# A two-layer graph network on one core: query blocks of 496 and 351, more products on GpSimd, second products split by columns

## The chip, the core and the metric

The kernel runs on one core of a Trainium2 chip. The metric is the device time of one execution in microseconds, the median of three runs. The engines are called by the profile's names: PE (TensorE, matrix products; PEld is its weight load), DVE (VectorE), ACT (ScalarE), POOL (GpSimd) and SP (SyncE, which here issues DMAs).

## The reference

There are N = 3327 nodes with D = 128 features and a dense 0/1 adjacency matrix `adj`. Layer 0 is a graph convolution with batch norm. Layer 1 is an attention in which the roles are unusual: each of the 128 columns d of the projections, reshaped, is an attention of its own with a head size of 8 over all 3327 nodes, and twice the adjacency matrix is added to the scores.

```python
h = jnp.maximum(_layernorm(x), 0.0)
x = x + layer0(h, adj)           # adj.T @ h / deg, two weights, batch norm, relu
h = jnp.maximum(_layernorm(x), 0.0)
q = (h @ Wq.T).reshape(d, n, 8)  # k and v likewise; d = 128, n = 3327
a = jnp.einsum('dnh,dmh->dnm', q, k) * d ** -0.5 + adj + adj
out = jnp.einsum('dnm,dmh->dnh', softmax(a, axis=2), v)
return x + out.reshape(n, 8 * d) @ Wo.T
```

So 128 attentions of 3327 x 3327 scores are computed, and nearly all the time is spent there.

## The kernel before

**Front.** The first 290 us compute layer 0, all in one pool of SBUF tiles (`l0`): 26 loads of rows of `adj` with seven products each, batch norm, `residual`, the second norm (`roots`, `factors`, `second_norm`, `columns`) and the projections of the first four heads (`project_now`). After these stand the loads of k, v and q of the first group; q goes over ACT's DMA queue (L578), k is sorted by casts on POOL and ACT (L581). Three early blocks of weights exp(2 adj + low) are made for the chunks from WC = 19 on (L433, `weigh_early`) and written to DRAM as `wd`.

**Attention.** NG = 32 groups of G = 4 columns d. A group goes over seven blocks of queries (six of 512 and one of 255), and a block over the 26 chunks of 128 keys. A chunk has two halves, each with two of the four heads, so a block has 52 pairs (chunk, half). They are handled in SU = 13 steps of four pairs. A pair's product `s` (L725) is two matrix products of K = 32 into one PSUM tile of two banks; there are three such tiles (`psc`). A pair is finished in one of two ways:

- plain (38 a block): DVE adds the adjacency tile to `s` (L818, `add`) into one part of the tile `d`; the whole `d` of a step, three pairs, is exponentiated by ACT one step later (L856, `late`).
- weighted (14 a block): ACT exponentiates `s` directly (L828), and POOL multiplies the result `f` with the weights from `wd` (L831).

A step has three plain pairs and a weighted one; the last has two of each. Three steps later (LAG) the second products (L604, `weigh`) multiply the exponentials with v and gather in the PSUM tile `av`. They are fp32, with 9 columns each, and four of them for four heads stand in the four column groups of PE; each shows as two records. `second(0)` issues the couple of the first two pairs, `second(1)` that of the others. The order on PE, written out by hand, is in each step: weighted product, first plain product, `second(0)`, a part of `finish` (the end of the block before), second and third plain product, `beside`, `second(1)`.

**Beside the loop.** `beside` puts nine parts of side work into the steps of each group: six projections for a later group (`projection`) and three parts of the output of the group before (`outputs`). Each has a PE part (steps 7 and 10), an evacuation by DVE (8 and 11) and a last part (9 and 12). `more_weights` makes the weights of the blocks from 3 on within the first group. `loads` spreads the loads of the next group's q, k and v over SP's queue and its sorting casts over POOL.

Which of the three `s` tiles a product takes is settled when the program is built: the one that is expected to be free first. Names of the engines' waits in the built program show the choice.

Of the kernel before, what the change touches and what calls it, by code (L numbers as in the profile page):

```python
# [44 lines left out]
def tile_two_layer_gnn(  # L45
# [21 lines left out]
    }))  # L67
    blocks = [(n0, min(NB, N - n0)) for n0 in range(0, N, NB)]

    const = ctx.enter_context(tc.tile_pool(name="const", bufs=1))  # L70
# [57 lines left out]

    def q_loads(q, p0, d):

        qs = qT[:, bass.ds(d * N, NP)].rearrange("(a h) n -> a h n", h=H)
        return [(q[p0 + i * H : p0 + (i + 1) * H].bitcast(F32), qs[i // 2]) for i in range(4)]

# [152 lines left out]
    with tc.tile_pool(name="l0", bufs=1) as l0, tc.tile_pool(  # L286
# [50 lines left out]
        def roots(c0, c1):  # L337
            nc.scalar.activation(sd[:, c0:c1], mv[:, c0:c1, 1], AF.Sqrt, bias=eps)
# [93 lines left out]
        weights = []  # L432
        for y, (n0, w) in enumerate(blocks[:EARLY]):  # L433
            a = ap.tile([P, 7 * NB], F32, name="a")
            a7 = a.rearrange("p (c n) -> p c n", c=7)
            nc.sync.dma_start(a7[:, :, :w], adjr[:, WC:, n0 : n0 + w])
            weights.append((a7, n0, w))

        def weigh_early():
            a7, n0, w = weights.pop(0)  # L440
            nc.scalar.activation(a7[:, :, :w], a7[:, :, :w], AF.Exp, bias=low, scale=2.0)
            nc.sync.dma_start(
                wd[:, :, n0 : n0 + w].rearrange("c p n -> p c n"), a7[:, :, :w]
            )

# [71 lines left out]
        def residual(i):  # L517
            pt, cs = turned(i, A, acc[i])
            nc.vector.tensor_add(xs[:, cs, :], xs[:, cs, :], pt)
            nc.sync.dma_start(  # L520
                xd.rearrange("(c p) d -> p c d", p=P)[:, cs, :], xs[:, cs, :]
            )

# [52 lines left out]
        for i in range(4, NQ):  # L576
            relu(i)
        for b in range(G):  # L578
            for args in q_loads(q, 32 * b, b):
                nc.scalar.dma_start(*args)  # L580
        for x, c in enumerate(range(0, NC, 4)):  # L581
            n = min(4, NC - c)
            (nc.scalar.copy if x % 2 else nc.gpsimd.tensor_copy)(
                k[:, c : c + n, :],
                ks.bitcast(F32).rearrange("g (p c) -> g c p", c=NC)[:, c : c + n, :],
            )
# [10 lines left out]
        keep_columns(0, NQ)  # L597
        weigh_early()

# [9 lines left out]
    def finish(rp, av, d0, n0, w):  # L609

        avs = rp.tile([P, NB], F32, name="avs")
        nc.vector.tensor_copy(avs[:, :w], av[:, :w])  # L612
        yield

        J = 4 if w == NB else 3
# [36 lines left out]
    def attention():  # L652


        with tc.tile_pool(name="adj", bufs=4) as ap, tc.tile_pool(
# [17 lines left out]
            if True:  # L673
                steps = [
                    (i, y, s)
                    for i in range(NG) for y in range(len(blocks)) for s in range(SU)
                ]
# [4 lines left out]
                def pairs(s):  # L682


                    last = s == SU - 1
                    plain = [(j // 2, j % 2) for j in range(3 * s, 3 * s + 3 - last)]
                    rest = [(WC + s // 2, 1 - s % 2)]
                    return plain, rest + ([(NC - 1, 0)] if last else [])


                wanted, have = [], {}
                for x, (i, y, s) in enumerate(steps):
                    n0, w = blocks[y]
# [4 lines left out]
                    c = pairs(s)[1][0][0]  # L698
                    if (1, i, y, c) not in have:
                        have[1, i, y, c] = None  # L700
                        wanted.append((x, 1, i, y, c))

                def fetch(x):
                    while wanted and wanted[0][0] <= x:
                        _, kind, i, y, c = wanted.pop(0)
                        n0, w = blocks[y]
                        if kind:
# [10 lines left out]
                def product(i, y, c, half):  # L718
                    q, k, _ = sets[i % 2]
                    n0, w = blocks[y]  # L720
                    we = w + w % 2
# [8 lines left out]

                waiting, ending, pending = [], [], []
                late = None

                def more_weights(i, y, s):

                    k, phase = s // 3, s % 3
                    if i or y + 1 >= len(blocks) or y + 1 < EARLY or k > 3:
                        return
                    n0, w = blocks[y + 1]
                    c = WC + 2 * k  # L740
# [33 lines left out]
                extra = []  # L774

                def second(part):

                    (i, y, s), es = waiting[0]
                    n0, w = blocks[y]
                    av = avs2[(i * len(blocks) + y) % 2]  # L780
# [8 lines left out]
                    if part:  # L789
                        waiting.pop(0)  # L790
                        if s == SU - 1:
                            ending.append(finish(rp, av, at(i), n0, w))

# [5 lines left out]
                for x, (i, y, s) in enumerate(steps):  # L799
                    n0, w = blocks[y]  # L800
                    fetch(x + PRE)
                    k = x - i * SU * len(blocks) - FROM[i]
# [4 lines left out]
                    while pending and (total - len(pending)) * (SU * len(blocks) - FROM[i] - 4) <= k * total:  # L807
# [42 lines left out]
                    beside(i, y, s)  # L850
                    if due:
                        second(1)

# [4 lines left out]
                    waiting.append(((i, y, s), es))  # L858
                late()
                while waiting:  # L860
                    second(0)
                    step()
                    second(1)
                while ending:
# [6 lines left out]
    def attention_shifted():  # L871

        with tc.tile_pool(name="shq", bufs=1) as shp, tc.tile_pool(
# [11 lines left out]
            with tc.For_i(0, D, G) as d0:  # L885
# [3 lines left out]
                for b in range(G):  # L889
# [3 lines left out]
                    )  # L893
                for y, (n0, w) in enumerate(blocks):
                    we = w + w % 2
# [168 lines left out]
```

## Time and profile before

| | us |
|---|---|
| median of three runs (10510.94 to 10513.17) | 10511.22 |
| profiled execution, as timed | 10527.91 |
| its span in the profile | 10526.1 |
| first DVE addition of the attention | 298.15 |
| start of one wide block's copy of `av` to that of the next (L612), without and with two parts of side work | 46.95 and 48.33 |
| one group (five starts of L612 from 4953.84 to 5271.93, seven blocks apart) | 318.09 |
| DMA, mean busy share of 16 engines in that group | 57% |
| granted PE clock, mean | 0.986 |

A line of the timeline has a start, a length (both in us), the engine, the line of the code, the operation, output and input tiles with their shapes, and how many equal instructions were merged; the brackets hold idle time before it and what ended it. A pipelined engine starts an instruction before the one ahead has fully ended, so what an instruction costs its engine is read from start to start. PE records' ends are modelled.

### The profile page before, as it was taken

The numbers are of one execution on the slowest core, as the hardware profiler recorded it, in microseconds if no ns is written. First come the engines' busy times: TensorE is split into PE (matmuls) and PEld (weight loads), VectorE is DVE, ScalarE is ACT, GpSimd is POOL, SyncE is SP. The second block draws the span as 40 slices with busy tenths as digits, with TensorE's granted clock in tenths as the row PEclk, the third lists the DMA queues.
The fourth block names the chain that finished last, engine by engine and source line by source line (L and its number), as shares of the span: only waits on it lengthen the run. The fifth ranks groups of instructions, "written<-read, shape, count | busy, mean of one in ns | idle before, by whom it ended". The sixth has DMA issues, their size and how long they took to land. (4 is left out here: it accounts for less than half of the span.)

```text
span 10526.1 us, 186778 instructions
## 1 busy us (share of the span) xinstructions
PE 9922.7 (94%) x72399; PEld 2813.8 (27%) x72399; DVE 9714.9 (92%) x9949; ACT 9948.5 (95%) x6200; POOL 7497.1 (71%) x3868
## 2 busy tenths in 40 slices
PE   7889999999999999999999999999999999999999
PEld 3222222222222222222222222222222222222222
DVE  5789999999999999999999999999999999999998
ACT  4889999999999999999999999999999999999998
POOL 0667777777777777777777777777777777777776
PEclk8899999999999999999999999999999999999999
DMA  7655555555555555555555555555555555555554
GB/s 241 192 168 163 157 168 165 163 162 160 162 166 165 164 162 157 161 170 163 160 162 157 165 170 165 160 158 163 164 169 163 162 163 158 165 165 167 156 152 128
DMA packets 1115761, 1731.67 MB, mean 165 GB/s; under 512 B 198350, under 2 KB 441932, under 8 KB 1107180
## 3 DMA queue, kind: packets, MB, share of 16 engines
q1 hardware_dynamic: 1110478, 1713.99, 56.3%
q8 instruction: 568, 9.31, 0.4%
q10 hardware_dynamic: 4350, 5.64, 0.2%
q14 instruction: 333, 2.73, 0.1%
q0 software_dynamic: 32, 0.00, 0.0%
HBM read 1618.76 MB, written 100.53 MB: 163 GB/s over the span
## 5 line engine op out<-in xcount | busy, mean ns | idle before, releaser
L818 DVE SCALAR_TENSOR_TENSOR d<-at,s 128x1024 f32<-128x1024 f32 x8512 | 9204.3, 1138 | 642.7 <-PE s L725 406.2
L831 POOL TENSOR_TENSOR f<-f,wt 128x1024 f32<-128x1024 f32 (+1 forms) x3136 | 6983.8, 2235 | 2619.1 <-ACT f L828 2572.0
L856 ACT ACTIVATE d<-d 128x3072 f32<-128x3072 f32 (+1 forms) x2912 | 7372.9, 2532 | 73.4 <-DVE d L818 70.5
L604 PE MATMUL av<-d,v 128*9 128x512 f32 x34048 | 5528.5, 569 | 0.1
L725 PE MATMUL s<-q,k 32*128 32x512 f32 x23296 | 4280.7, 482 | 505.7 <-DVE d L818 218.0
L725 PEld LDWEIGHTS s<-q,k 32*128 32x128 f32 x23296 | 1773.9, 182 | 5829.2 <-DVE d L818 3312.2
L828 ACT ACTIVATE f<-s 128x1024 f32<-128x1024 f32 (+1 forms) x3136 | 3014.8, 970 | 313.8 <-PE s L725 252.3
L604 PE MATMUL av<-f,v 128*9 128x512 f32 x12544 | 2864.0, 571 | 0.0
L604 PEld LDWEIGHTS av<-d,v 128*9 128x9 f32 x34048 | 630.7, 88 | 1381.6 <-issue 1265.4
L604 PEld LDWEIGHTS av<-f,v 128*9 128x9 f32 x12544 | 310.6, 88 | 52.9 <-issue 41.0
L180 POOL CAST k<-ks 128x256 fp32r<-128x256 f32 x434 | 284.2, 655 | 0.0
L416 PE MATMUL acc<-a,A 128*128 128x512 f32 (+1 forms) x364 | 151.3, 568 | 24.0 <-ACT A L350 23.3
L619 PEld LDWEIGHTS av<-ident,avs 128*128 128x128 f32 (+1 forms) x864 | 121.1, 208 | 179.9 <-issue 178.8
L226 POOL TENSOR_TENSOR o<-pf,o 104x512 fp32r<-104x512 f32 x124 | 160.4, 1293 | 9.9
L619 PE MATMUL av<-ident,avs 128*128 128x128 f32 (+1 forms) x864 | 163.8, 311 | 0.6 <-DVE avs L612 0.6
L225 POOL CAST o<-pf 104x512 fp32r<-104x512 f32 x124 | 75.8, 611 | 115.3 <-DVE pf L224 59.8
L612 DVE COPY avs<-av 128x512 f32<-128x512 f32 (+1 forms) x224 | 144.2, 644 | 2.8 <-PE av L604 2.8
L423 DVE TENSOR_REDUCE amax<-a 128x1 f32<-128x3327 f32 x26 | 93.7, 3610 | 37.7 <-DMA a<-in_adj 37.7
L416 PEld LDWEIGHTS acc<-a,A 128*128 128x128 f32 x364 | 68.8, 192 | 108.8 <-issue 84.4
L420 ACT ACTIVATE junk<-a 128x3327 bf16<-128x3327 f32 x26 | 77.4, 2977 | 6.6 <-DMA a<-in_adj 6.5
L389 POOL TENSOR_TENSOR sq<-wk 128x512 f32<-128x512 f32 x2 | 2.1, 1040 | 102.3 <-PE aside L390 102.3
L629 DVE TENSOR_TENSOR oq<-av,ri 128x128 f32<-128x128 f32 (+1 forms) x224 | 64.1, 286 | 7.7
(120 smaller groups left out, 952.0 us busy)
## 6 DMA issues: line engine op xcount, KB each, us to landing
at<-in_adjT SPq DMA_DIRECT2D x1728, 512.0 KB
wt<-wd SPq DMA_DIRECT2D x1344, 256.0 KB
at<-in_adjT SPq DMA_DIRECT2D x288, 255.0 KB
ks<-kT SPq DMA_DIRECT2D x496, 104.0 KB
q<-qT SPq DMA_DIRECT2D x496, 104.0 KB
at<-in_adjT SPq DMA_DIRECT2D x192, 256.0 KB
a<-in_adj SPq DMA_DIRECT2D x26, 1663.5 KB
wt<-wd SPq DMA_DIRECT2D x224, 127.5 KB
```

What stands on the lines that cost most here:

```text
L180: nc.gpsimd.tensor_copy(k[:, c : c + n, half * 64 : half * 64 + 64], ks.bitcast(F32).rearrange("g (p c) -> g c p", c=NC)[:, c : c + n, :],)
L226: nc.gpsimd.tensor_tensor(o[:CH, 1], f[:CH], o[:CH, 0].bitcast(F32), ALU.subtract)
L416: nc.tensor.matmul(acc[i][:, :w], A[:, c, :], a[:, n0 : n0 + w], start=(c == 0), stop=(c == NC - 1),)
L423: nc.vector.tensor_reduce(amax[:, c : c + 1], a[:, :N], AX.X, ALU.max, apply_absolute_value=True)
L604: nc.tensor.matmul(av[32 * b : 32 * b + H + 1, :w], tiles[2][:, b, c, :], e, start=first, stop=last,)
L612: nc.vector.tensor_copy(avs[:, :w], av[:, :w])
L619: nc.tensor.transpose(pt[:R, j, :], avs[:, j : j + (R - 1) * J + 1 : J], ident)
L725: nc.tensor.matmul(p[:, x, :we], k[rs, c, :], q[rs, n0 : n0 + we], start=True, stop=True,)
L818: nc.vector.scalar_tensor_tensor(d[:, j, :, :w], have[0, i, y, c // 2][:, c % 2, :w] .unsqueeze(1).to_broadcast([P, 2, w]), SAFE / 2, p[:, ...
L828: nc.scalar.activation(f[:, :, :w], p[:, :, :w], AF.Exp, scale=2.0)
L831: nc.gpsimd.tensor_tensor(f[:, :, :w], f[:, :, :w], have[1, i, y, c][:, :w].unsqueeze(1).to_broadcast([P, 2, w]), ALU.mult,)
L856: nc.scalar.activation(flat, flat, AF.Exp, scale=2.0)
```

## The change

- Queries go in blocks of QB = 496, so six of 496 and one of 351 (`qblocks`) instead of six of 512 and one of 255. Layer 0 keeps its blocks.
- WC is 18: 16 of the 52 pairs are weighted and 36 plain. Steps 4, 8 and 12 (`DOUBLE`) have two weighted pairs, the others one.
- A couple of second products is split by columns into two halves of 248 where a block is wider than `NARROW` = 400. The first half of the first couple stands where that couple stood; its second half and both halves of the second couple stand behind the step's last product.
- Front: only one block's weights are made early, in two halves; the others are made in the first group by `more_weights`. Only the first 512 queries are loaded in front; the rest of q is loaded by SP, two DMAs a step, in the first eight steps (`others`). The sorting casts of k stand behind `columns`, the last `weigh_early` moved up, and `xs` is stored once instead of in seven parts.
- Side work: the PE part in steps 7 and 11, the evacuation in 8 and 12, the last part in 9 or in step 0 of the next block.

```diff
+QB = 496
-WC = 19
+WC = 18
-EARLY = 3
+DOUBLE = (4, 8, 12)
+NARROW = 400
...
-        for y, (n0, w) in enumerate(blocks[:EARLY]):
+        for n0 in range(0, NB, NB // 2):
             a = ap.tile([P, 7 * NB], F32, name="a")
-            a7 = a.rearrange("p (c n) -> p c n", c=7)
-            nc.sync.dma_start(a7[:, :, :w], adjr[:, WC:, n0 : n0 + w])
-            weights.append((a7, n0, w))
+            a8 = a[:, : 8 * (NB // 2)].rearrange("p (c n) -> p c n", c=8)
+            nc.sync.dma_start(a8, adjr[:, WC:, n0 : n0 + NB // 2])
+            weights.append((a8, n0, NB // 2))
...
+
         for b in range(G):
-            for args in q_loads(q, 32 * b, b):
+            for args in q_loads(q, 32 * b, b, 0, NB):
                 nc.scalar.dma_start(*args)
-        for x, c in enumerate(range(0, NC, 4)):
...
+        nc.sync.dma_start(xd.rearrange("(c p) d -> p c d", p=P), xs)
...
-        weigh_early()
+        for x, c in enumerate(range(0, NC, 4)):
...
+                kinds = []
+                for s in range(SU):
+                    j, k = (sum(len(x[i]) for x in kinds) for i in range(2))
+                    n = 2 if s in DOUBLE else 1
+                    kinds.append((
+                        [(x // 2, x % 2) for x in range(j, j + 4 - n)],
+                        [(WC + x // 2, 1 - x % 2) for x in range(k, k + n)],
+                    ))
...
-                    if i or y + 1 >= len(blocks) or y + 1 < EARLY or k > 3:
+                    if i or y + 1 >= len(qblocks) or k > 3:
                         return
...
-                    if s in (8, 11) and extra:
+                    if s in (8, 12) and extra:
                         drive(extra[0])
-                    if s in (9, 12) and extra:
+                    if s == 9 and extra or s == 0 and (y or i) and begun:
                         drive(extra.pop(0))
+                        begun.pop()
-                    if s in (7, 10) and extra:
-                        drive(extra[0], avs2[(i * len(blocks) + y + 1) % 2])
+                    if s in (7, 11) and extra:
+                        begun.append(1)
+                        drive(extra[0], avs2[(i * len(qblocks) + y + 1) % 2])
...
+                def second(part, half):
+                    h = w // 4 * 2 if w > NARROW else w
+                    n0, n1 = (0, h) if half == 0 else (h, w)
                     for j in (0, 1) if part == 0 else (2, 3):
+                        if n0 == n1:
+                            break
-                        c, half = ps[j]
+                        c, b = ps[j]
                         for x in range(2):
                             weigh(
-                                sets[i % 2], av, w, es[j][:, x, :w], 2 * half + x, c,
-                                s == 0 and part == 0, s == SU - 1 and part == 1,
+                                sets[i % 2], av[:, n0:n1], n1 - n0, es[j][:, x, n0:n1],
+                                2 * b + x, c, s == 0 and part == half == 0,
+                                s == SU - 1 and part == 1 and n1 == w,
                             )
...
+                    for args in others[:2]:
+                        nc.sync.dma_start(*args)
+                    del others[:2]
...
                     add(0, product(i, y, *plain[0]))
-                    if due:
-                        second(0)
+                    second(0, 0)
                     step()
                     add(1, product(i, y, *plain[1]))
...
                     beside(i, y, s)
-                    if due:
-                        second(1)
+                    second(0, 1)
+                    second(1, 0)
+                    second(1, 1)
```

More of the change, by code (lines that the diff above doesn't have):

```diff
@@ L68, in tile_two_layer_gnn @@
     blocks = [(n0, min(NB, N - n0)) for n0 in range(0, N, NB)]
+    qblocks = [(n0, min(QB, N - n0)) for n0 in range(0, N, QB)]
     const = ctx.enter_context(tc.tile_pool(name="const", bufs=1))
@@ L127, in tile_two_layer_gnn, with q_loads @@
     sets = [tile_set(x) for x in range(2)]
-    def q_loads(q, p0, d):
-        qs = qT[:, bass.ds(d * N, NP)].rearrange("(a h) n -> a h n", h=H)
-        return [(q[p0 + i * H : p0 + (i + 1) * H].bitcast(F32), qs[i // 2]) for i in range(4)]
+    def q_loads(q, p0, d, n0=0, n=NP):
+        qs = qT[:, bass.ds(d * N + n0, n)].rearrange("(a h) n -> a h n", h=H)
+        return [
+            (q[p0 + i * H : p0 + (i + 1) * H, n0 : n0 + n].bitcast(F32), qs[i // 2])
+            for i in range(4)
+        ]
     def k_loads(k, p0, d, n0, n):
@@ L432, in tile_two_layer_gnn @@
         weights = []
-        for y, (n0, w) in enumerate(blocks[:EARLY]):
+        for n0 in range(0, NB, NB // 2):
             a = ap.tile([P, 7 * NB], F32, name="a")
-            a7 = a.rearrange("p (c n) -> p c n", c=7)
-            nc.sync.dma_start(a7[:, :, :w], adjr[:, WC:, n0 : n0 + w])
-            weights.append((a7, n0, w))
+            a8 = a[:, : 8 * (NB // 2)].rearrange("p (c n) -> p c n", c=8)
+            nc.sync.dma_start(a8, adjr[:, WC:, n0 : n0 + NB // 2])
+            weights.append((a8, n0, NB // 2))
         def weigh_early():
[L440 to L444, printed above, removed]
+            a8, n0, w = weights.pop(0)
+            nc.scalar.activation(a8, a8, AF.Exp, bias=low, scale=2.0)
+            nc.sync.dma_start(wd[:, :, n0 : n0 + w].rearrange("c p n -> p c n"), a8)
         top = l0.tile([P, 1], F32, name="top")
@@ L519, in residual @@
             nc.vector.tensor_add(xs[:, cs, :], xs[:, cs, :], pt)
-            nc.sync.dma_start(
-                xd.rearrange("(c p) d -> p c d", p=P)[:, cs, :], xs[:, cs, :]
-            )
         def second_norm(i, engine):
@@ L578, in tile_two_layer_gnn @@
         for b in range(G):
-            for args in q_loads(q, 32 * b, b):
+            for args in q_loads(q, 32 * b, b, 0, NB):
                 nc.scalar.dma_start(*args)
-        for x, c in enumerate(range(0, NC, 4)):
[L582 to L586, printed above, removed]
         for i in range(2, NQ):
@@ L597, in tile_two_layer_gnn @@
         keep_columns(0, NQ)
-        weigh_early()
+        for x, c in enumerate(range(0, NC, 4)):
+            n = min(4, NC - c)
+            (nc.scalar.copy if x % 2 else nc.gpsimd.tensor_copy)(
+                k[:, c : c + n, :],
+                ks.bitcast(F32).rearrange("g (p c) -> g c p", c=NC)[:, c : c + n, :],
+            )
     def weigh(tiles, av, w, e, b, c, first, last):
@@ L613, in finish @@
         yield
-        J = 4 if w == NB else 3
+        J = 4 if w == QB else 3
         R = w // J
@@ L675, in attention @@
                     (i, y, s)
-                    for i in range(NG) for y in range(len(blocks)) for s in range(SU)
+                    for i in range(NG) for y in range(len(qblocks)) for s in range(SU)
                 ]
@@ L682, in pairs @@
                 def pairs(s):
[L685 to L688, printed above, removed]
+                    return kinds[s]
+                kinds = []
[6 more added lines that the diff above has]
+                    ))
                 wanted, have = [], {}
                 for x, (i, y, s) in enumerate(steps):
-                    n0, w = blocks[y]
+                    n0, w = qblocks[y]
                     for c, _ in pairs(s)[0]:
@@ L697, in attention @@
                             wanted.append((x, 0, i, y, c // 2))
[L698 to L701, printed above, removed]
+                    for c, _ in pairs(s)[1]:
+                        if (1, i, y, c) not in have:
+                            have[1, i, y, c] = None
+                            wanted.append((x, 1, i, y, c))
                 def fetch(x):
@@ L705, in fetch @@
                         _, kind, i, y, c = wanted.pop(0)
-                        n0, w = blocks[y]
+                        n0, w = qblocks[y]
                         if kind:
@@ L719, in product @@
                     q, k, _ = sets[i % 2]
-                    n0, w = blocks[y]
+                    n0, w = qblocks[y]
                     we = w + w % 2
@@ L731, in attention @@
                 waiting, ending, pending = [], [], []
+                others = [
+                    args for b in range(G)
+                    for args in q_loads(sets[0][0], 32 * b, b, NB, NP - NB)
+                ]
                 late = None
@@ L736, in more_weights @@
                     k, phase = s // 3, s % 3
-                    if i or y + 1 >= len(blocks) or y + 1 < EARLY or k > 3:
+                    if i or y + 1 >= len(qblocks) or k > 3:
                         return
-                    n0, w = blocks[y + 1]
+                    n0, w = qblocks[y + 1]
                     c = WC + 2 * k
@@ L771, in beside @@
+                    if s in (7, 11) and extra:
+                        begun.append(1)
+                        drive(extra[0], avs2[(i * len(qblocks) + y + 1) % 2])
                     if (y, s) == (2, 12) and i:
                         extra.extend(outputs(wk, i - 1))
-                extra = []
-                def second(part):
+                extra, begun = [], []
+                def second(part, half):
+                    if not due:
+                        return
                     (i, y, s), es = waiting[0]
-                    n0, w = blocks[y]
-                    av = avs2[(i * len(blocks) + y) % 2]
+                    n0, w = qblocks[y]
+                    av = avs2[(i * len(qblocks) + y) % 2]
@@ L788, in second @@
                             )
-                    if part:
+                    if part and half:
                         waiting.pop(0)
                         if s == SU - 1:
-                            ending.append(finish(rp, av, at(i), n0, w))
+                            ending.append(finish(rp, av, at(i), qblocks[y][0], w))
                 def step():
@@ L799, in attention @@
                 for x, (i, y, s) in enumerate(steps):
-                    n0, w = blocks[y]
+                    n0, w = qblocks[y]
                     fetch(x + PRE)
-                    k = x - i * SU * len(blocks) - FROM[i]
+                    k = x - i * SU * len(qblocks) - FROM[i]
                     if k == 0 and i + 1 < NG:
@@ L805, in attention @@
                         total = len(pending)
-                    while pending and (total - len(pending)) * (SU * len(blocks) - FROM[i] - 4) <= k * total:
+                    while pending and (total - len(pending)) * (SU * len(qblocks) - FROM[i] - 4) <= k * total:
                         pending.pop(0)()
                     more_weights(i, y, s)
+                    for args in others[:2]:
+                        nc.sync.dma_start(*args)
+                    del others[:2]
                     due = len(waiting) == LAG
@@ L859, in attention @@
                 late()
+                due = True
                 while waiting:
-                    second(0)
+                    for j in range(4):
+                        second(j // 2, j % 2)
                     step()
-                    second(1)
                 while ending:
@@ L893, in attention_shifted @@
                     )
-                for y, (n0, w) in enumerate(blocks):
+                for y, (n0, w) in enumerate(qblocks):
                     we = w + w % 2
```

## The prediction

> **What bounds the kernel now.** I read the shares and the instruction groups by form, then the waits, then the timeline of single steps. Groups (count | busy us, mean ns | idle before):
>
> ```profile
> PE 9922.7 (94%) x72399; PEld 2813.8 (27%) x72399; DVE 9714.9 (92%) x9949; ACT 9948.5 (95%) x6200; POOL 7497.1 (71%) x3868
> L818 DVE SCALAR_TENSOR_TENSOR d<-at,s 128x1024 f32<-128x1024 f32 x7296 | 8417.5, 1213 | 474.6 <-PE s L725 270.4 <-issue 98.4 <-ACT d L856 23.7
> L831 POOL TENSOR_TENSOR f<-f,wt 128x1024 f32<-128x1024 f32 x2688 | 6412.7, 2394 | 2343.2 <-ACT f L828 2303.0 <-DMA q<-qT 19.8 <-DMA wt<-wd 14.6
> L856 ACT ACTIVATE d<-d 128x3072 f32<-128x3072 f32 x2304 | 6398.3, 2777 | 60.4 <-DVE d L818 59.1 <-ACT f L828 0.2
> L828 ACT ACTIVATE f<-s 128x1024 f32<-128x1024 f32 x2688 | 2753.2, 1032 | 239.1 <-PE s L725 211.8 <-POOL k L180 12.6 <-POOL f L831 7.2
> ```
>
> Three engines stand above 90%, so shares decide nothing. Waits (total us, times, longest):
>
> ```profile
> PEld s L725 <- ACT f L828: 1197.0, 1922, 11.8
> ACT f L828 <- PE s L725: 252.3, 380, 7.6
> ACT d L856 <- DVE d L818: 70.5, 212, 0.6
> ```
>
> TensorE waits for ScalarE's exponential f, and ScalarE waits for TensorE's s: a loop. Call a step's four products R (the weighted one, to f) and P0, P1, P2. ScalarE around a block's end, where the last step has two weighted products:
>
> ```profile
> 4938.14 1.02 ACT L828 ACTIVATE f<-s 128x1024 f32<-128x1024 f32 x1
> 4939.04 2.77 ACT L856 ACTIVATE d<-d 128x3072 f32<-128x3072 f32 x1
> 4941.70 1.94 ACT L828 ACTIVATE f<-s 128x1024 f32<-128x1024 f32 x2
> 4943.50 1.93 ACT L856 ACTIVATE d<-d 128x2048 f32<-128x2048 f32 x1
> 4945.69 1.02 ACT L828 ACTIVATE f<-s 128x1024 f32<-128x1024 f32 x1 [0.26 <-PE s L725]
> ```
>
> Starts give what each holds ScalarE: 0.90 us for f, 2.66 for d, so an ordinary step is 3.56 us and ScalarE sets it without a gap. Only the step behind the double one shows 0.26 us of idle time. The loop of such a step, in another block:
>
> ```profile
> 5163.11 1.94 ACT L828 ACTIVATE f<-s 128x1024 f32<-128x1024 f32 x2
> ...
> 5165.10 0.50 PE L725 MATMUL s<-q,k 32*128 32x512 f32 x2 [0.42 <-ACT f L828]
> 5165.53 0.60 PE L604 MATMUL av<-d,v 128*9 128x512 f32 x2
> ...
> 5166.51 0.51 PE L725 MATMUL s<-q,k 32*128 32x512 f32 x4
> ```
>
> The second f began near 5164.02. P2 takes R's PSUM buffer, so it starts 1.08 us after f's start; the second products begin 0.43 later, and last 0.98; behind them comes the next R, whose f starts 0.60 later where ScalarE is free (5155.38 to 5155.98). Sum 3.09 us: the 3.09 from 4942.60 to 4945.69. In an ordinary step the loop has 3.56 - 3.09 = 0.47 us to spare.
>
> **What the Trainium skill says.** "PSUM — Partial Sum Buffer", Engine vs sequencer instructions: matrix products start and complete in order, only weight loads run ahead. The trace agrees: TensorE stands at P2 although second products are ready. "ScalarE: Activation LUTs", What ACT_TABLE_LOAD costs: 186 ns + 0.833 ns per element with immediates, neighbours overlapping by 93 ns; 1024 elements give 1039 ns against 1032 measured. "TensorE: Matmul & The Clock Gate", Back-to-back issue gap: about 25 ns from start to start however short the product. The quarters come close to that, so the drain, where second products follow each other without anything between, matters:
>
> ```profile
> 10502.41 0.39 PE L604 MATMUL av<-d,v 128*9 128x255 f32 x2
> ...
> 10502.84 0.61 PE L604 MATMUL av<-d,v 128*9 128x255 f32 x8
> ...
> 10503.27 0.39 PE L604 MATMUL av<-f,v 128*9 128x255 f32 x2
> ```
>
> Three couples of 255 columns begin 0.43 us apart, without a fixed cost for each. A couple of 512 takes 0.98 when alone: 0.86 of columns and 0.12 to change over.
>
> **The change, part by part.** All per group of four heads (32 groups; starts of the steps show 318.1 us for one, of which 28.3 is the block of 255).
>
> *Blocks of 496 and 351.* Seven blocks before and after, so no fixed cost goes. At 0.833 ns an element, f holds ScalarE 0.873 us at 496 and d 2.58. Six blocks lose 16 columns and one gains 96: 52 pairs x 2 x 96 x 0.833 ns = 8.3 us of ScalarE move. But the block of 255 was bound by its loop (2.02 us a step; E to P2 0.67, products 0.32, second products 0.55, to the next f 0.48), not by ScalarE (1.86). At 351 the loop scales to 2.42 and ScalarE to 2.49: seven ordinary steps 17.4, three double 9.4, three behind them 6.2, and 1.5 of the 2.2 us of stray waits that the block has now: 34.5. So it pays 6.2 and the wide ones get 8.3.
>
> *16 of 52 pairs on GpSimd.* VectorE drops 2 x 1.12 us a block and falls far below ScalarE. GpSimd rises to 16 x 2.33 = 37 us of 47 and stays hidden. ScalarE does all 52 exponentials either way (+0.1 us). What goes: ScalarE's waits for VectorE, about 0.45 us a block where a finished block is drained (2.7 a group), and evacuations now fit into double steps. What comes: three double steps a block instead of one.
>
> *Couples split by columns.* The order R P0, couple, P1 P2, couple becomes R P0, half a couple, P1 P2, three halves. P1 comes sooner to VectorE, which no longer needs it. Behind P2 stands 0.12 + 3 x 0.413 = 1.36 us instead of 0.98. The loop at 496: 1.05 + 0.41 + 1.36 + 0.585 = 3.41 us, ScalarE's ordinary step 0.873 + 2.58 = 3.45. Ordinary steps stay bound by ScalarE with 0.04 us to spare. The step behind a double one holds ScalarE only 0.873 + 1.755 = 2.63 and now takes 3.41: 0.78 us lost, three times a block. In the changed program's order the fourth product waits for ScalarE there in every wide block. A wide block: 7 x 3.45 + 3 x 4.33 (two f, one d) + 3 x 3.41 = 47.4; six, 284.3. Before, by the same count, 11 x 3.56 + 4.46 + 3.09 = 46.7, plus side work.
>
> *Side work behind P2* (nine parts a group: six projections, two turns, one output sum). A projection puts 1.01 us on TensorE (0.54 lost now, with 0.47 spare), a turn 0.51, the output sum some 2.04 (16 products of 0.128). With 0.04 spare nearly all shows: 5.8 + 0.9 + 2.0 = 8.7 us, against 5.0 before. VectorE's copies moved to steps 8 and 12 cost nothing there; without that slack 0.45 each.
>
> Sum: 284.3 + 8.7 + 0.9 (half of the 1.8 that my count of before leaves unexplained) + 34.5 = 328.4, against 318.1: +10.3 us, in 31 groups +319.
>
> *Front and first group.* Query loads drop from 16 x 104 KB to 16 x 16 KB, and ScalarE's queue was held by them from 233.8 to 270.3 us, with roots, norms and columns behind. One early write less, casts behind the columns, one store of xs instead of seven. The first add (298.15) should come near 276, then held by the landing of the hd store and the first adjacency tiles: -22, bounds -30 and -5. Against it two more blocks of the first group make weights inside: 4 x 1.04 us of ScalarE and a first wait for the load of 3.3 to 4.1 (seen once in each such block) each: +16, bounds +8 and +24. The remaining query loads put 16 issues of about 0.5 us on SP's queue in eight steps, beside two or three others a step: hidden; if not, the adjacency loads behind them come 1 us late. The first group's share of the above counts +8, as it has stalls that hide some.
>
> Total 10526.1 + 319 + 8 - 22 + 16 = 10847 as span; the profiled execution (10527.91) is 16.7 above the median, so **10830** (+3.0%).
>
> **Rivals.**
> 1. *Split halves cost a changeover each* (+0.12 x 2, the issue limit of the skill page): loop 3.65 us, above ScalarE's. Ten steps a block then lose 0.2 to 0.24: +2.2 us a block, +13 a group, about 11250. For: 26 ns an instruction, close to the limit. Against: the drain.
> 2. *The loop costs half of it:* f starts sooner behind R, or part of the side work hides: +4 a group, 10640. For: buffers alternate between steps now. Against: 0.26 idle is seen with less behind P2.
> 3. *Faster: the loop opens.* Place: P2 behind a double step. If P2 found a buffer that VectorE has freed (some steps now do this), the three halves would run under ScalarE, and only ScalarE's floor remained: 6 x 45.04 + 32.5 + 4 = 307, -11 a group, near 10150. It decides once the step behind the double one falls below about 2.7 us. Against: the changed order names ScalarE's f there.
>
> **How the numbers follow.** Forecast 0.62 (10700 to 10970), rival 1 0.16, rival 2 0.12, rival 3 0.07, no change (within 0.2%, what a measurement here can tell) 0.03. Unknown costs: 0.1 us on the loop is 6 us a group, 190 in all; finish waits that stay, +85. The range 10630 to 11060 takes in the forecast, rival 2 and the lower part of rival 1. Faster 0.08, same 0.03, slower 0.89.
>
> **What would show it.** Right: d exponentials back to back, yet f waiting for s by about 0.7 us three times a wide block; the total of f waiting for s rising from 252 to over 700 us; ScalarE waiting for VectorE near nothing; groups of about 328 us. Wrong: ordinary steps above 3.5 us (rival 1), or f behind a double step without idle time (rival 3).

## The result, and the profile after

| | us |
|---|---|
| changed kernel, median of 4 runs (10999.49 to 11038.71) | 11025.98 |
| kernel before, beside it, median of 4 runs (10510.94 to 10520.04) | 10512.19 |
| ratio, with its 95% interval | 1.0484 (1.0464 to 1.0504) |
| forecast | 10830 (10630 to 11060) |

The change makes the kernel 4.8% slower; 3.0% was forecast. The profiled execution took 10999.49 us, its span is 10997.7. First the busy shares (share of the span), from the page of the changed kernel:

```profile
PE 9875.3 (90%) x112335; PEld 3788.0 (34%) x112335; DVE 9361.4 (85%) x9501; ACT 9980.7 (91%) x6655; POOL 8461.3 (77%) x4316
```

PE and ACT have about the busy time that they had before (9922.7 and 9948.5 us), in a span that is 472 us longer. So the work of these two did not grow; they stand idle more. ACT's groups by form (count | busy us, mean ns | idle before them) say where:

```profile
L882 ACT ACTIVATE d<-d 128x2976 f32<-128x2976 f32 x1920 | 5159.7, 2687 | 0.0
L854 ACT ACTIVATE f<-s 128x992 f32<-128x992 f32 x3072 | 2999.1, 998 | 762.4 <-PE s L734 746.0 <-POOL f L857 14.5 <-issue 0.2
L882 ACT ACTIVATE d<-d 128x1984 f32<-128x1984 f32 x576 | 1083.3, 1881 | 0.0
```

The exponentials d of the wide blocks never wait. All the idle time of the wide blocks stands in front of f, and it ends with the product s: 746 us, where it was 212. The waits (total us, times, longest) show the same pair of engines from both sides:

```profile
PEld s L734 <- ACT f L854: 2073.3, 3022, 2.7
...
PE s L734 <- ACT f L854: 959.3, 2622, 2.0
ACT f L854 <- PE s L734: 796.1, 953, 3.4
```

PE waits for f, and f waits for PE: the loop of the prediction. ACT's timeline around a double step (f x2, then the short d) and a projection:

```profile
5047.30 1.90 ACT L854 ACTIVATE f<-s 128x992 f32<-128x992 f32 x2
5049.05 1.90 ACT L882 ACTIVATE d<-d 128x1984 f32<-128x1984 f32 x1
5051.64 1.00 ACT L854 ACTIVATE f<-s 128x992 f32<-128x992 f32 x1 [0.69 <-PE s L734]
...
5059.57 1.00 ACT L854 ACTIVATE f<-s 128x992 f32<-128x992 f32 x1 [0.90 <-PE s L734]
```

And PE in the same stretch:

```profile
5049.25 0.49 PE L734 MATMUL s<-q,k 32*128 32x496 f32 x2 [0.39 <-ACT f L854]
5049.68 0.80 PE L607 MATMUL av<-d,v 128*9 128x248 f32 x10
...
5051.05 0.49 PE L734 MATMUL s<-q,k 32*128 32x496 f32 x4
```

The second f of the pair begins 0.87 us behind the first, near 5048.17. P2 begins 1.08 later (5049.25), the halves 0.43 after it, the next R 1.37 after these, the next f 0.59 after that: 3.47 us for the loop, where ACT has 2.63 us of work. The 0.69 in brackets is not the whole loss: without a wait the f starts 1.75 us behind the short d (the median in `e_nosplit`), here 2.59. With a wait, two neighbours also lose the 0.12 to 0.15 us by which they otherwise overlap here; this is more than the 93 ns that the prediction names.

From end to end, the mean of 31 groups (start to start of the narrow block's copy of `av`) went from 316.96 to 333.02 us: +498 us in all. The way to the end of the first group became 25.4 us shorter (680.2 to 654.8).

### The profile page after: what moved, and what is told of

Its sections match the earlier page's. It is cut to its first block, busy times and chain, and to the rows that moved or that the text cites. A ratio compares the mean times of both kernels' runs of the same rounds, so it can differ in the third digit from the quotient of the medians.

```text
span 10997.7 us, 267650 instructions
## 1 busy us (share of the span) xinstructions
PE 9875.3 (90%) x112335; PEld 3788.0 (34%) x112335; DVE 9361.4 (85%) x9501; ACT 9980.7 (91%) x6655; POOL 8461.3 (77%) x4316
## 5 line engine op out<-in xcount | busy, mean ns | idle before, releaser
L844 DVE SCALAR_TENSOR_TENSOR d<-at,s 128x992 f32<-128x992 f32 x8064 | 8830.0, 1140 | 1497.0 <-PE s L734 1086.4
L857 POOL TENSOR_TENSOR f<-f,wt 128x992 f32<-128x992 f32 (+1 forms) x3584 | 7958.3, 2235 | 2266.3 <-ACT f L854 2255.8
L882 ACT ACTIVATE d<-d 128x2976 f32<-128x2976 f32 (+1 forms) x2912 | 7002.7, 2405 | 12.2 <-DVE d L844 11.5
L607 PE MATMUL av<-d,v 128*9 128x248 f32 x59904 | 5301.4, 387 | 0.3 <-ACT d L882 0.3
L734 PE MATMUL s<-q,k 32*128 32x496 f32 x23296 | 4097.3, 483 | 1054.5 <-ACT f L854 959.3
L854 ACT ACTIVATE f<-s 128x992 f32<-128x992 f32 (+1 forms) x3584 | 3369.5, 963 | 813.7 <-PE s L734 796.1
L607 PE MATMUL av<-f,v 128*9 128x248 f32 x26624 | 2926.3, 387 | 0.0
L607 PEld LDWEIGHTS av<-d,v 128*9 128x9 f32 x59904 | 1447.2, 90 | 2213.6 <-issue 1475.1
L607 PEld LDWEIGHTS av<-f,v 128*9 128x9 f32 x26624 | 1072.1, 92 | 244.7 <-issue 19.3
L622 PE MATMUL av<-ident,avs 128*124 128x128 f32 (+1 forms) x864 | 165.0, 312 | 0.7 <-DVE avs L615 0.7
```

Source lines behind the costliest of these rows:

```text
L607: nc.tensor.matmul(av[32 * b : 32 * b + H + 1, :w], tiles[2][:, b, c, :], e, start=first, stop=last,)
L622: nc.tensor.transpose(pt[:R, j, :], avs[:, j : j + (R - 1) * J + 1 : J], ident)
L734: nc.tensor.matmul(p[:, x, :we], k[rs, c, :], q[rs, n0 : n0 + we], start=True, stop=True,)
L844: nc.vector.scalar_tensor_tensor(d[:, j, :, :w], have[0, i, y, c // 2][:, c % 2, :w] .unsqueeze(1).to_broadcast([P, 2, w]), SAFE / 2, p[:, ...
L854: nc.scalar.activation(f[:, :, :w], p[:, :, :w], AF.Exp, scale=2.0)
L857: nc.gpsimd.tensor_tensor(f[:, :, :w], f[:, :, :w], have[1, i, y, c][:, :w].unsqueeze(1).to_broadcast([P, 2, w]), ALU.mult,)
```

## The experiments

Twelve kernels ran. In the table, "group" is the mean of the 31 groups after the first. "Wide" and "narrow" are what six wide blocks and one narrow block hold ACT, from the start of their first f to that of the first f behind them (means of groups 2 to 31). "Half clock" counts the stretches of 3.4 or 6.8 us, between 700 and 10150 us, in which the trace shows PE's granted clock at 0.5. Six kernels have no split, with `NARROW = 1000` as in `e_nosplit`, beside what is shown of their edits: `e_qb512_whole`, `e_between`, `e_shift`, `e_best`, `e_own_r` and `e_own_r_shift`.

| kernel | us | ratio to before (95%) | group | wide | narrow | half clock |
|---|---|---|---|---|---|---|
| before | 10512.19 | 1 | 316.96 | 288.22 | 29.14 | 23 |
| changed | 11025.98 | 1.0484 (1.0464 to 1.0504) | 333.02 | 297.89 | 35.66 | 85 |
| e_before_split | 10736.63 | 1.0208 (1.0191 to 1.0225) | 323.65 | 293.96 | 30.12 | 34 |
| e_one_double | 10629.14 | 1.0104 (1.0087 to 1.0121) | 320.31 | 285.37 | 35.42 | 19 |
| e_couple_back | 10534.36 | 1.0016 (1.0010 to 1.0023) | 317.69 | 283.13 | 34.93 | 8 |
| e_nosplit | 10384.85 | 0.9873 (0.9857 to 0.9890) | 313.05 | 278.45 | 34.97 | 0 |
| e_qb512_whole | 10456.75 | 0.9944 (0.9927 to 0.9961) | 315.74 | 286.69 | 29.42 | 15 |
| e_between | 10357.73 | 0.9851 (0.9834 to 0.9867) | 312.44 | 277.96 | 34.85 | 0 |
| e_shift | 10395.50 | 0.9886 (0.9870 to 0.9903) | 312.99 | 278.37 | 34.97 | 0 |
| e_best | 10415.39 | 0.9906 (0.9889 to 0.9922) | 313.56 | 279.11 | 34.85 | 0 |
| e_three_first | 10821.20 | 1.0286 (1.0269 to 1.0303) | 327.21 | 287.61 | 39.94 | 0 |
| e_own_r_split | 11044.31 | 1.0502 (1.0484 to 1.0519) | 334.44 | 298.00 | 36.86 | 0 |
| e_own_r | 10515.21 | 1.0001 (0.9992 to 1.0010) | 317.66 | 282.38 | 35.68 | 0 |
| e_own_r_shift | 10593.05 | 1.0075 (1.0058 to 1.0092) | 319.68 | 284.46 | 35.69 | 0 |

**Two halves behind P2 instead of three.**

```diff
                     second(0, 0)
+                    second(0, 1)
...
                     beside(i, y, s)
-                    second(0, 1)
                     second(1, 0)
```

> The split stays, but the second half of the first couple goes back in front of P1; two halves instead of three stand behind P2. Loop theory: the loop of a step behind a double one falls from 3.41 to about 2.99 us against 2.63 of ScalarE, so f waits there about 0.3 us instead of 0.69, and an ordinary step has 0.46 us to spare, which hides half of a projection (0.90 idle to about 0.45). Group 333.5 to about 322, time 10610 to 10690. Rival, the split instructions themselves cost the time: nothing about them changes, so 10950 to 11030. Rival, TensorE's clock: only a few us, unless the drops go with the loop.

Moving one half took 492 us away, nearly all of the loss. ACT behind a double step:

```profile
5008.04 1.87 ACT L882 ACTIVATE d<-d 128x1984 f32<-128x1984 f32 x1
5010.19 1.00 ACT L854 ACTIVATE f<-s 128x992 f32<-128x992 f32 x1 [0.28 <-PE s L734]
```

The gap is 0.28 where 0.3 was expected and 0.69 stood. That is 0.41 us less, the time of the one half that was moved. By group, the waits of f in wide blocks fell from 16.0 to 5.4 us behind double steps and from 8.0 to 4.4 elsewhere. The time came out 76 us below the range. PE's half-clock stretches went from 85 to 8, which had not been counted on; the waits that they lengthen (see below) account for about 3.7 us a group of it. The split instructions are all still there: they are not the cost by themselves.

**No split.**

```diff
-NARROW = 400
+NARROW = 1000
```

> No couple is split; the whole first couple stands in front of P1, the whole second one behind P2, as before the change; blocks and 16 of 52 pairs stay. Loop theory: the same loop as in e_couple_back, but in 341 of 556 wide steps behind a double one the fourth product takes a buffer that VectorE freed, so no wait there; 10480 to 10620, some 70 to 100 us below e_couple_back, and where the buffer is R's the same wait of about 0.3 us. Rival, halves cost a changeover each: more than 200 us below e_couple_back, and the loop itself shorter by 0.12 us or more in steps with the same buffers.

150 us below `e_couple_back`, more than the loop theory said and less than the changeover rival; the time itself lies 95 us below the forecast range. The wait decides:

```profile
5050.48 1.89 ACT L882 ACTIVATE d<-d 128x1984 f32<-128x1984 f32 x1
5052.65 1.00 ACT L854 ACTIVATE f<-s 128x992 f32<-128x992 f32 x1 [0.27 <-PE s L734]
```

Where the buffer is R's, whole couples leave 0.27 us and halves 0.28: a half costs no changeover. What differs is how often: 7 waits behind double steps in the wide blocks of a group here, 18 there, since the built program gives P2 another buffer than R's in 341 of 556 such steps. 11 waits of 0.30 us and 0.12 of lost overlap are 4.6 us, which is the difference of the groups (317.69 - 313.05).

**One double step, split kept.**

```diff
-WC = 18
-DOUBLE = (4, 8, 12)
+WC = 19
+DOUBLE = (12,)
...
```

> 14 of 52 pairs on GpSimd with one double step a block, as before the change; blocks of 496, the split and the three halves behind P2 stay. Loop theory: two losses of 0.69 us a wide block go, and two exponentials f: 8 to 10 us a group, 10700 to 10780; one gap of 0.69 a wide block and the 0.90 behind a projection remain. Rival, more pairs on GpSimd cost nothing and the split alone does: within 60 us of 11026. Rival, VectorE (38 adds of 1.14 us, 43.5 of about 46 us a wide block) is late again: ScalarE waits for VectorE by more than 70 us in all.

12.7 us a group came back, more than the 8 to 10 expected, and the time lies 71 us below the range: twelve waits behind double steps (16.0 to 4.8 us of idle time a group and 12 x 0.12 of overlap), in which the half-clock stretches (85 to 19) are contained. The 0.9 behind side work stayed (8.0 to 7.9 us a group). VectorE was late for only 16 us in all.

**The split alone, on the kernel before.** The halves and their order as in the change, nothing else.

```diff
-                    if due:
-                        second(0)
+                    second(0, 0)
...
-                    if due:
-                        second(1)
+                    second(0, 1)
+                    second(1, 0)
+                    second(1, 1)
```

> The kernel before with one part of the change alone: couples split by columns, half a couple in front of P1 and three halves behind P2; blocks of 512 and 255 and one double step a block stay. Loop theory: the loop goes from 3.09 to 1.08 + 0.43 + 1.41 + 0.60 = 3.52 us against ScalarE's 3.56, so the wait behind a double step grows from 0.26 to about 0.7 (six a group) and that behind a projection from 0.4 to about 0.9 (nine pieces of side work): 6 to 7 us a group, 10690 to 10750. Rival, only the double steps make it slow and the split alone is harmless: 10480 to 10550. Rival, each half costs a changeover: ordinary steps above 3.56 us, over 10850.

As forecast in time, in the group (+6.7) and in the gap, here at a block's one double step:

```profile
5032.86 1.94 ACT L863 ACTIVATE d<-d 128x2048 f32<-128x2048 f32 x1
5035.49 1.02 ACT L835 ACTIVATE f<-s 128x1024 f32<-128x1024 f32 x1 [0.69 <-PE s L725]
```

So the split's order costs 6.7 us a group with one double step a block (widths of 512 and 255), and 20.0 (333.02 - 313.05) with three (496 and 351). The double steps cost 12.7 with the split; without it they bring a small gain (`e_qb512_whole` against before, 315.74 to 316.96, side work moved as well). So most of the loss comes from the two edits together.

**Block widths alone, without the split.**

```diff
-QB = 496
+QB = 512
```

> e_nosplit with blocks of 512 and 255 queries instead of 496 and 351; all else as there. By the prediction's sum, the narrow block is bound by its loop at 255 and by ScalarE at 351, and the new blocks save some 2 us a group: so 10420 to 10460 here. Rival, the widths are worth nothing: 10365 to 10405. Rival, the new widths cost (more work in the narrow block than it hides): below 10350.

10456.75: the widths 496 and 351 are worth 72 us. The narrow block pays 34.97 - 29.42 = 5.6 us and the wide ones get 8.2 (forecast 6.2 and 8.3).

**Three halves in front of P1, one behind P2.**

```diff
                     second(0, 0)
+                    second(0, 1)
+                    second(1, 0)
...
-                    second(0, 1)
-                    second(1, 0)
                     second(1, 1)
```

> The split stays, but three halves stand between P0 and P1 and one behind P2. Loop theory: in the steps behind a double one the loop is 1.05 + 0.41 + 0.48 + 0.585 = 2.53 us, below ScalarE's 2.63, so no wait is left there; in ordinary steps it is P1 that takes R's buffer, 2.94 us against 3.45. Group 313 to 317, time 10390 to 10520, at or below the kernel before. Rival, TensorE's own work is the bound once the loop is open: its busy share above 95% and 10550 to 10650. Rival, VectorE gets P1 too late: ScalarE's d waits for VectorE by more than 150 us, above 10650.

My forecast failed, and the VectorE rival named in it held; that of PE's own work did not, with a busy share of 89%. ACT around a double step:

```profile
5019.13 2.69 ACT L882 ACTIVATE d<-d 128x2976 f32<-128x2976 f32 x1 [0.30 <-DVE d L844]
...
5025.58 1.00 ACT L854 ACTIVATE f<-s 128x992 f32<-128x992 f32 x1 [0.25 <-PE s L734]
5027.01 2.69 ACT L882 ACTIVATE d<-d 128x2976 f32<-128x2976 f32 x1 [0.43 <-DVE d L844]
```

Behind the double step f waits little, but now d waits for VectorE: 282.5 us in all, against 11.5 in the changed kernel. P1 and P2 come only after three halves, and each has an addition of 1.14 us to go before d can start. In the narrow block, whose couples are whole, both stand in front of P1, and it grew to 39.94. Second products are late work behind P2 and early work in front of P1; there is a price on each side.

**Whole couples, the second one in front of P2 behind double steps.**

```diff
                     add(1, product(i, y, *plain[1]))
+                    early = (s - 1) % SU in DOUBLE
+                    if early:
+                        for j in (1, 2, 3):
+                            second(j // 2, j % 2)
...
                     beside(i, y, s)
-                    second(0, 1)
-                    second(1, 0)
-                    second(1, 1)
+                    if not early:
+                        for j in (1, 2, 3):
+                            second(j // 2, j % 2)
```

> e_nosplit with one thing moved: in the steps behind a double one the whole second couple goes in front of P2, so that behind P2 only the next R stands. Loop theory: the loop there is 1.05 + 0.41 + 0.585 = 2.05 us against 2.63 of ScalarE; the 7 waits of 0.27 us a group in e_nosplit (with 0.12 of lost overlap each) go: 2.8 us a group, 10280 to 10330. Rival, VectorE then gets P2 too late, as in e_three_first: ScalarE's d waits for VectorE, and the time is above 10385.

The waits of f behind double steps are gone in the wide blocks (7 a group to none), as the loop theory has it, but VectorE takes most of it back in the wide blocks, as the rival has it, since P2 comes later: d waits for it 1.3 us a group, where it did not, and starts 0.91 us behind f in place of 0.88 on average, sixty times a group. What is left are 0.6 us a group and 3 in the first group, 27 us in all below `e_nosplit`; the time lies between the forecast and what the rival named. This is the fastest version of all, 1.5% below the kernel before.

**Side work moved into the double steps**, with that order (`e_best`) and without (`e_shift`); its copies and last parts move one step later with it.

```diff
...
-                    if s in (7, 11) and extra:
+                    if s in (8, 12) and extra:
```

> e_between, and TensorE's part of the side work (projections, turns, output sum) moves from the steps 7 and 11 into the double steps 8 and 12, where ScalarE has 4.33 us of work and TensorE 0.9 us to spare; its copies and stores move one step later with it. Loop theory: the seven waits behind side work of e_nosplit (4.3 us a group and 0.8 of lost overlap) go as well: group 305 to 308, 10150 to 10230. Rival, TensorE has no room there: the waits only move into the steps behind the double ones, 10280 to 10330.

> e_nosplit with TensorE's part of the side work moved into the double steps 8 and 12, and the couples left in their old places (e_best without e_between). Here the fourth product takes R's buffer in 482 of 556 wide steps behind a double one, against 215 in e_nosplit. Loop theory: the side work's waits go (4.3 + 0.7 us a group), 8.6 more waits of 0.27 + 0.12 us come: 1.6 us a group net, 10320 to 10350. Rival, it is the moved side work and not the moved couple that made VectorE late in e_best: above 10400.

Both missed: `e_shift` lies between its forecast and its rival, `e_best` above both of its own. In both the waits behind side work went (4.3 to 0.5 us a group), so the room in the double steps is real. But the program's choice of buffers changed with the order: the fourth product behind a double step takes R's buffer in 482 of 556 wide steps, against 215. In `e_shift` that gives 16 waits of 0.29 us a group for 7, and d follows f by 0.90 in place of 0.88 us: groups equal to those of `e_nosplit`. In `e_best`, P2 is then late for VectorE as well, and d follows f by 0.99 us. Both also have a longer first group: it ends 21 and 17 us later than in `e_nosplit` (674.1 and 670.5 against 653.1); why was not looked into.

**R in a PSUM buffer of its own**, P0, P1 and P2 in the other two.

```diff
-tc.tile_pool(name="psc", bufs=3, space=PSUM) as psc
+tc.tile_pool(name="psc", bufs=2, space=PSUM) as psc
+tc.tile_pool(name="psr", bufs=1, space=PSUM) as psr
...
-                    weighted(*rest[0])
+                    weighted(*rest[0], psr)
```

> The changed kernel, split and three halves behind P2 kept, but R has a PSUM buffer of its own and P0, P1, P2 (and the second R of a double step) share the other two; P2 then always takes a buffer that VectorE has emptied, as in the prediction's third rival. Loop theory: f no longer holds P2; the waits of 0.69 us and more behind the double steps go although the instructions are the same, and with them TensorE's half-clock windows: 16 to 20 us a group, 10400 to 10560. Rival, a loop through VectorE takes its place (P2 waits for the add of P0, some 0.25 us in every step, in the split order): 10650 to 10860. Rival, the split itself is slow: 10950 or more.

> e_nosplit with R in a PSUM buffer of its own. Loop theory: the seven waits a group behind double steps (0.27 us and 0.12 of overlap each) go, and the side work has the whole of ScalarE's step to hide in: group 306 to 310, 10170 to 10290. Rival, two buffers are too few for VectorE's adds, so that they start late and ScalarE's d waits for VectorE: above 10385.

> e_own_r with TensorE's part of the side work in the double steps, as in e_best. Loop theory: side work that still shows in e_own_r goes: at or up to 120 us below e_own_r. Rival, two buffers too few: above 10385, ScalarE's d waiting for VectorE.

These were to open the loop without touching the instructions, and they show what it is exchanged for. PE in two ordinary steps of `e_own_r_split`:

```profile
5059.94 0.61 PE L607 MATMUL av<-d,v 128*9 128x248 f32 x8
...
5061.40 0.49 PE L736 MATMUL s<-q,k 32*128 32x496 f32 x2 [0.43 <-DVE d L846]
5061.82 0.61 PE L607 MATMUL av<-d,v 128*9 128x248 f32 x8
...
5063.19 0.50 PE L736 MATMUL s<-q,k 32*128 32x496 f32 x4
```

P2 now waits 0.43 us for VectorE to empty P0's buffer, in ordinary steps too, and the three halves stand behind that. A step takes 3.68 us (ACT's f starts at 5060.10 and 5063.78) instead of 3.45. So no half-clock stretches, smaller waits behind double steps (mostly 0.3 to 0.5), and yet the time of the changed kernel: the VectorE loop of the rival, nearly twice as dear as I had put it. Without the split the same exchange costs 130 us (`e_own_r` against `e_nosplit`), and 198 with the side work moved (`e_own_r_shift` against `e_shift`). All three missed their forecasts. In the two without the split the rival's number held, but not its way: d does not wait for VectorE. PE does (60.9 us in `e_nosplit`, 300.8 in `e_own_r`, 475.0 in `e_own_r_shift`), and f then waits for s. That the split is harmless once the loop is open could therefore not be shown in this way; `e_couple_back` against `e_nosplit` shows only that a half costs nothing more in the same loop.

## Why the prediction was right, and where it fell short

*The mechanism* was right: a loop f, P2, second products, R, f that ScalarE's short step behind a double one cannot cover. d exponentials run back to back, f waits 0.69 us three times a wide block (404 of 493 such waits in 29 groups; a loss of 0.84 with the overlap, 0.78 forecast), the total of f waiting for s is 796 us (over 700 forecast), ACT's waits for VectorE fell from 70.5 to 11.5 us. Ordinary steps stayed at 3.45 us: rival 1 falls, and the equal gaps of `e_couple_back` and `e_nosplit` say so again. Rival 2 (half of the loss) and rival 3 (an open loop) fall with the 0.69.

*The size* was not: 11026 us lies inside the range but above the 10700 to 10970 that were held most likely, and a group lost 16.1 us instead of 10.3.

*Side work*: forecast 8.7 us a group, measured 8.0 of idle time and about 0.9 of overlap. *Narrow block*: forecast +6.2 us, measured +6.5 (29.14 to 35.66). Both levels were about 1 us too low in the sum. In that of the new block, 6.2 us for three steps behind double ones is less than three turns of its own loop of 2.42 us; the two of them that end inside the block take 2.46 and 2.18.

*The term that was too small* is the six wide blocks with their side work: forecast 293.9 us a group, measured 297.89. The shortest of the 30 measured took 293.79, so the sum describes a group that nothing else disturbs. The rest is a thing that the sum did not have: PE's granted clock. Of these 493 waits, the 86 long ones are 1.8 to 2.5 us instead of 0.69, and the trace's clock was at half speed just ahead of every one of them, and of none of the 404. One case; the windows give the stretch, its length, then busy us (instructions) of PE, PEld, DVE, ACT and POOL, the granted clock, the DMA share and GB/s:

```profile
838.90:842.30 3.40, 2.38 (x28) 0.80 (x24) 2.39 (x3) 3.40 (x4) 2.27 (x2) 1.00 0.55 160
842.30:845.70 3.40, 3.40 (x32) 1.15 (x28) 1.47 (x3) 1.29 (x2) 3.15 (x2) 0.50 0.41 106
```

and what PE and ACT do there:

```profile
842.16 1.30 PE L607 MATMUL av<-d,v 128*9 128x248 f32 x10
...
844.66 0.79 PE L734 MATMUL s<-q,k 32*128 32x496 f32 x4
...
845.54 1.00 ACT L854 ACTIVATE f<-s 128x992 f32<-128x992 f32 x1 [2.11 <-PE s L734]
```

From the three halves to the next R it is 2.50 us here, not 1.37. The 86 long waits exceed 0.69 by some 1.36 us on average: 86 x 1.36 / 29 = 4.0 us a group, as much as lies between 293.9 and 297.89, and about 125 us in all. A stretch at half clock costs this much because it falls on the chain that sets the time. In the kernel before, only 6 of the 22 in the same groups lengthened a wait behind a double step. Such stretches become fewer with the waits of the loop (85, then 8 in `e_couple_back` and none in `e_nosplit`), so the waits seem to cost a second time, through the clock; that they bring it about is not shown (see the last section).

*The kernel before* was put 0.7 us too long in total (318.1, where groups 2 to 31 have 317.4) and 1.6 too long in its wide blocks with side work (289.8 counted, 288.22 measured), which took another 1.6 us from the difference. So +10.3 became about +16: 4.0 of clock, 1.6 from that count and 0.3 from the narrow block.

*Front and first group* erred the other way. The first addition came at 274.31 us, 23.8 earlier (forecast 22). From there to the end of the first group +24 us was forecast, and -1.6 measured (382.1 to 380.5). `e_one_double`, with the same front but 14 weighted pairs, took 403.4 from its first addition (273.9): +21, close to the forecast. So what failed is the term that put more weighted pairs into the first group as a loss: there, two more pairs on GpSimd were worth some 23 us, and the split made no difference (381.2 from the first addition in `e_nosplit`). By what way stays open: between 500 and 650 us f waits for s 37.0 us in `e_one_double` and 13.0 in the changed kernel, and between 350 and 650 the clock of PE is 0.90 there and 0.97 here, though `e_nosplit` has 0.93 and the same short way. This error of some 27 us stands against that of the groups, so by chance it brought the total nearer to the forecast.

The sum, measured: +498 in 31 groups, -25 to the end of the first group, -1 behind the last one, +472 of span.

## What to carry to other kernels

Where one engine's product reuses a buffer that another engine must first read, everything queued between that product and the next thing the reader needs is part of a loop; compare the loop with the shortest step of the reader, not with the average one. Two edits can cost far more together than apart: here one lengthened the loop (2.1% alone) and the other, which gained a little without it, made three times as many short steps of that reader. When a reordering is tried, look again at which buffer each product takes in the built program, since that moved with some of the orders here and explains the difference between `e_couple_back` and `e_nosplit`, and why `e_shift` gained nothing.

## What the runs showed of the hardware

The Trainium skill ("TensorE: Matmul & The Clock Gate", What's actually happening) describes a free-running window of 3413 ns and half clock after an idle window. The 3.413 us grid agrees: the starts of all 85 half-clock stretches of the changed kernel lie on it. But no idle window was needed: the window ahead of each had PE busy for 2.37 to 2.47 of 3.41 us, counted with the modelled ends of its products, and no gap longer than 0.64. Between 700 and 10150 us, 307 windows at full clock had at most 2.47 us, and 85 of them were followed by half clock; of the 2375 busier ones none was. Yet low busy time alone does not decide it either: `e_three_first` has 86 windows of at most 2.47 us and no half clock, and in the kernel before the drops follow windows of 2.69 to 2.87. What decides it was not settled.
